# A graph layer on one core: the first edge layer as eight products of 32 rows and 64 columns, and 386 picked tiles instead of 376

## The chip, the core and the metric

The kernel runs on one core of a Trainium2 chip. A core has TensorE (matrix products, results in PSUM), VectorE (DVE), ScalarE (ACT), GpSimd (POOL) and queues that move data by DMA; each engine works through its own instructions in order and waits for others by semaphores. The metric is the device time of one execution in microseconds (us). Before the change it is 1485.16 us, the median of 7 runs (1483.39 to 1488.86).

## What is computed

```python
def ref(features, edge_index, edge_attr, edge_sh, c_noise, W1, b1, W2, b2, W_tp, ...):
    src, dst = edge_index                                    # 200000 edges, 6250 nodes, dst sorted
    w = silu(edge_attr @ W1 + b1) @ W2 + b2                  # 32 -> 64 -> 9 numbers an edge
    h_src = features[src]                                    # 64 numbers an edge
    msg = einsum('ef,em,fmg->eg', h_src, edge_sh * w, W_tp)
    agg = segment_sum(msg, dst, num_segments=N) / sqrt(AVG_DEG)
    gamma, beta = split(silu(c_noise[:, None] @ Wn1 + bn1) @ Wn2 + bn2, 2)
    return agg * (1.0 + gamma) + beta
out = layernorm(x + ref(x, ...))
```

## The kernel before

The 200000 edges are 1563 tiles of 128, in 98 groups of 16 tiles (`NBLK`, `KB`). The main loop runs over `i`, and works on several groups at once, each at another stage. The order of each engine's instructions is written out by hand: they stand as the code calls them.

**Features of the source nodes (`hs`).** A group needs 16 x 128 rows of `x`. Most tiles are fetched by `gather` (line 97): one indirect DMA a tile on POOL's queue (line 99), six groups ahead, into seven buffers. In each fourth group from 7 on one tile is fetched by SP, 128 single row copies (`load_rows`, line 107). The last `picked(g)` tiles of a group are not fetched at all but selected on TensorE out of a copy of `x` in SBUF: `hots` (line 533) builds one-hot matrices on DVE from keys in PSUM (which `keys`, line 528, copies on ACT), `pick` (line 540) multiplies them in 14 products into `px` (line 552), and DVE multiplies by a mask (line 561) and sums (line 563) into `hs`. `picked(g)` is 4, or 3 where `g` is a multiple of 6 below 96: 376 tiles in all, beside 23 by SP and 1164 gathers.

**Weights of the edges.** `hidden` (line 476) is the first layer: `ea` holds a group's edge attributes as 4 x 32 rows by 512 columns. Two products take 64 rows each, by a block-diagonal `w1bd` of two copies of `W1`, into the two banks of the PSUM tile `p1` (line 481). `hidden_act` takes the Silu of both banks in one activation (line 490) into `st`. `second` (line 494) is the second layer, four products with 32 output columns side by side (line 499) and an addition of the bias on ACT (line 502). `weights` (line 504) turns the result on DVE, multiplies by `sh` (line 513) and spreads it over seven windows of nodes into `a` (line 519).

**Edge sums.** `windows` (line 571) multiplies `hs` by `a`, tile by tile, 16 products of 64 columns in two halves of eight (line 585), each half into a PSUM tile `pz` of tag "pz" with two buffers; 252 of a bank's 512 columns are used. The first of these products waits for all gathers of the group. ACT copies the sums out (line 596). `project` (line 618) multiplies pairs of groups by `W_tp` into the PSUM tile that shares the tag "p1" with the first layer (line 632), turns the result (line 638) and splits it in two parts (lines 606, 607); `nodes` (line 666) with `place`, `bring`, `gate` and `finish` adds them up to nodes, in PSUM of tag "s", which `second` uses too.

**Order of an iteration.** `gather(i+6)`, loads, `keys(i+2)`; `pick(i+1, 0)` with the parts of `nodes(i)` and `hots(i+2)` between its products; `hidden(i+2)` (line 724); `second(i+1)`; `windows(i)`; `project` in odd iterations; `pick(i+1, 1)` with `weights(i+1)`; a part of the nodes' end; `pick(i+1, 2)`; `pick(i+1, 3)`. In the setup `hidden(0)` to `hidden(2)` are called out of the loop, and the tag "pz" also serves some small products.

```python
                pick(i + 1, 0, [nodes(i), more])
                ...
                if i + 2 < NBLK:
                    hidden(i + 2)
                ...
                second(i + 1)
                windows(i)
```

Of the kernel before, what the change touches and what calls it, by code (L numbers as in the profile page):

```python
# [7 lines left out]
F32 = mybir.dt.float32  # L8
# [4 lines left out]
AF = mybir.ActivationFunctionType  # L13
# [3 lines left out]
P = 128  # L17
N, F, M, D, H, E = 6250, 64, 9, 32, 64, 200000
NJ = 49
NPAD = P * NJ  # L20
NT = (E + P - 1) // P
KB = 16
NBLK = (NT + KB - 1) // KB
W = 7
KW = KB * W
ZT = 8
FB = 2
AHEAD = 6
LB = 2
Q = 4  # L30
J = 7
SPS = 4
SPG = range(7, NBLK, SPS)
# [17 lines left out]

def picked(g):

    return Q - (g % 6 == 0 and g < NBLK - LB)


def tiles(g):
# [10 lines left out]
def gnn_resnorm_kernel(ctx: ExitStack, tc: tile.TileContext, x, src, dst, dst_row, ea, sh, cn,  # L68
                       w1, b1, w2, b2, wtp, wn1, bn1, wn2, bn2, out):
    nc = tc.nc  # L70
# [6 lines left out]
    w1bd = consts.tile([P, 2 * H], F32)  # L77
    b1c = even(consts, P, 1, F32, name="b1c")
# [8 lines left out]
    with ExitStack() as fast:  # L87
        loads = fast.enter_context(tc.tile_pool(name="loads", bufs=3))
        work = fast.enter_context(tc.tile_pool(name="work", bufs=2))
        gath = fast.enter_context(tc.tile_pool(name="gath", bufs=AHEAD + 1))  # L90
        keep = fast.enter_context(tc.tile_pool(name="keep", bufs=1))
        psum = fast.enter_context(tc.tile_pool(name="psum", bufs=1, space=bass.MemoryType.PSUM))
        late = fast.enter_context(tc.tile_pool(name="late", bufs=2))

        hs, hs_dma = {}, {}

# [22 lines left out]
        w2p = keep.tile([P, D], F32)  # L119
# [50 lines left out]
                lambda: nc.vector.scalar_tensor_tensor(jl[:, c0:c1], kh, -float(J) / P, rest,  # L170
                                                       op0=ALU.mult, op1=ALU.add)]

        def keys_turn(g0, kf, tag, kt):

            c0 = g0 * Q
            p_kt = psum.tile([P, P], F32, tag=tag, name=f"p_kt{g0}", bufs=1 + (tag == "pz"))
            nc.tensor.transpose(p_kt, kf, ident)
            nc.scalar.copy(kt, p_kt)
            return lambda: nc.sync.dma_start(kd[c0:c0 + P, :], kt)
# [9 lines left out]
        KC = P // Q  # L189
        KN = 10 * KB  # L190

        def setup(temp):
# [19 lines left out]
            for c in range(KB // 4):  # L212
                q = c * D
# [44 lines left out]
            one = temp.tile([1, 1], F32)  # L258
            nc.vector.memset(one, 0.0)

            def keys_first(g, kf, tag):

                pk_t[g] = psum.tile([P, Q, P], F32, tag=tag, name=f"pk{g}", bufs=1 + (tag == "pz"))
                spread = []
                for t in range(picked(g)):
                    c = (g + 1) * Q - picked(g) + t
                    d0 = NBLK * KB + c * P
                    dg = xb.rearrange("p j f -> p (j f)")[:, d0:d0 + P]
                    nc.vector.tensor_scalar(dg, ident, kf[:, c:c + 1], None, op0=ALU.mult)
                    spread.append(lambda t=t, dg=dg: nc.tensor.matmul(pk_t[g][:, t, :], ones, dg,  # L270
                                                                      start=True, stop=True))
                return spread
# [6 lines left out]
            kb = [ztw[:, k * LB * Q:(k + 1) * LB * Q] for k in range(6)]  # L279
            for f in keys_of(0, LB, kb):  # L280
                f()
            for f in keys_first(0, kb[0], "pz"):
                f()
            spread = keys_first(1, kb[0], "r")
            pw_i = temp.tile([P, 1], I32)
            nc.vector.tensor_scalar(pw_i, pf, 147.0, None, op0=ALU.mult)
            nc.vector.tensor_scalar(pw_i, pw_i, 10, None, op0=ALU.logical_shift_right)
# [22 lines left out]
            pick(0, 2)  # L310
            hidden(1, act=False)
            kt = temp.tile([P, P], F16)
            keys_turn(LB, kb[0], "pz", kt)()
            hidden_act(1)
            load_keys(LB)
            p_row = psum.tile([len(SPG), P], F32, tag="pz", name="p_row", bufs=2)
            nc.tensor.transpose(p_row, row_f, ident)
            hots(1, 1, 2)
            pick(1, 0)
            nc.vector.tensor_copy(row_a, p_row)  # L320
            nc.vector.tensor_sub(rel[:, 0:2 * KB], dst_i[:, 0:2 * KB], row_i)
            near(0)
            p_f = psum.tile([KB, NBLK], F32, tag="pz", name="p_f", bufs=2)
            nc.tensor.matmul(p_f, first_t, ident[0:NBLK, 0:NBLK], start=True, stop=True)
            nc.scalar.copy(first_f, p_f)
            p_cn = psum.tile([P, NJ], F32, tag="pz", name="p_cn", bufs=2)
            nc.tensor.matmul(p_cn, cn_j, ident[0:NJ, 0:NJ], start=True, stop=True)
            cn_s = temp.tile([P, NJ], F32)
            nc.scalar.copy(cn_s, p_cn)
# [13 lines left out]
            hots(1, 2, 3)  # L343
            pick(1, 1)
            nc.vector.tensor_copy(lo, lo_i)
            p_nid = psum.tile([P, NBLK], F32, tag="pz", name="p_nid", bufs=2)
            nc.tensor.matmul(p_nid, sel[0:KB], first_f, start=True, stop=True)
            nc.vector.scalar_tensor_tensor(nid, p_nid, pw, lo, op0=ALU.add, op1=ALU.subtract)
            windows(0)
# [126 lines left out]
        def hidden(g, act=True):  # L476

            e = ea_t.pop(g)
            p1 = psum.tile([P, 2, KB * P // 4], F32, tag="p1", name=f"p1_{g}")
            for i in range(2):  # L480
                nc.tensor.matmul(p1[:, i, :].rearrange("p (c t e) -> p c t e", c=4, t=4), w1bd[i * 64:(i + 1) * 64, :],  # L481
                                 e[i * 64:(i + 1) * 64, :].rearrange("p (t c e) -> p c t e", t=4, c=4),
                                 start=True, stop=True)
            p1_t[g] = p1
            if act:
                hidden_act(g)

        def hidden_act(g):
            st[g] = work.tile([P, 2, KB * P // 4], F32, tag="st", name=f"st{g}")
            nc.scalar.activation(st[g], p1_t.pop(g), AF.Silu, bias=b1c)  # L490

        p2, p2s = {}, {}

        def second(g):

            s = st.pop(g)
            p2[g] = psum.tile([P, 2, 2 * P], F32, tag="s", name=f"p2_{g}")
            for c in range(KB // 4):
                nc.tensor.matmul(p2[g][c * D:(c + 1) * D, 0, :].rearrange("p (i e) -> p i e", i=2), w2p,  # L499
                                 s[:, :, c * P:(c + 1) * P], start=True, stop=True)  # L500
            p2s[g] = work.tile([P, 2 * P], F32, tag="p2s", name=f"p2s{g}")
            nc.scalar.activation(p2s[g], p2[g][:, 0, :], AF.Identity, bias=b2c)  # L502

        def weights(g):

            p, v = p2.pop(g), p2s.pop(g)

            def part():
                nc.vector.transpose(p[:, 1, :], v)  # L509
                sw = p[:, 0, 0:KB * M].rearrange("p (t m) -> p t m", m=M)  # L510
                sh = sh_t.pop(g)
                for i in range(2):
                    nc.vector.tensor_mul(  # L513
                        sw[:, 8 * i:8 * i + 8].rearrange("p (s c) m -> p s c m", s=2),
                        p[:, 1, i * P:(i + 1) * P].rearrange("p (c q) -> p c q", q=D)[:, :, 0:2 * M]
                        .rearrange("p c (s m) -> p s c m", s=2),
                        sh[:, 8 * i:8 * i + 8].rearrange("p (s c) m -> p s c m", s=2))
                a[g] = work.tile([P, KB, M, W], F32, tag="a", name=f"a{g}")
                nc.vector.tensor_mul(a[g], oh_t.pop(g)[:, :, None, :].to_broadcast([P, KB, M, W]),  # L519
                                     sw.unsqueeze(3).to_broadcast([P, KB, M, W]))  # L520

            return [part]
# [48 lines left out]
        def windows(g, k0s=None):  # L571

            nk = tiles(g)
            end = g == NBLK - 1
            hsg, ag = hs[g], a[g]
            z = zs[g] if g in zs else sums(g)


            for k0 in range(0, nk, ZT) if k0s is None else k0s:
                n = min(ZT, nk - k0)  # L580
                pz = [psum.tile([P, ZT // 2, M, W], F32, tag="pz", name=f"pz{g}_{k0}", bufs=2)]
                pz.append(psum.tile([P, ZT // 2, M, W], F32, tag="px", name=f"pz{g}_{k0}_", bufs=2) if end else pz[0])
                for k in range(n):
                    v = k % 2
                    mm = nc.tensor.matmul(pz[v][v * F:(v + 1) * F, k // 2].rearrange("p m w -> p (m w)"),  # L585
                                          hsg[:, k0 + k, :], ag[:, k0 + k].rearrange("p m w -> p (m w)"),
                                          start=True, stop=True)
                    if k0 + k == 0:

                        for d in hs_dma.pop(g)[(g not in SPG):]:  # L590
                            tc.add_manual_dep(mm.ins, d.ins.name, mybir.DependencyInfo(
                                mybir.DependencyClass.Sync, mybir.DependencyReason.DATA), reason="rows of the group")
                for v in range(2):
                    copy = nc.vector.tensor_copy if end and k0 == ZT and v == 1 else nc.scalar.copy
                    for h in range(2):
                        copy(  # L596
                            z[h * F:(h + 1) * F, 0:5 - h, k0 + v:k0 + n:2, :].rearrange("p m k w -> p k m w"),
                            pz[v][v * F:(v + 1) * F, 0:(n + 1 - v) // 2, h:M:2, :])
# [91 lines left out]
        with tc.manual_schedule(), tc.tile_pool(name="temp", bufs=1) as temp:  # L690
# [6 lines left out]
            for i in range(1, NBLK):  # L697
# [22 lines left out]
                    hots(i + 2, 2, Q)  # L720
                if 56 <= i <= 58:
                    reach(i - 56)
                if i + 2 < NBLK:
                    hidden(i + 2)
                if i == NBLK - 2:
                    break
                second(i + 1)
# [9 lines left out]
                for t in range(2, Q + 1):  # L737
                    for f in beside[(t - 2) * n:(t - 1) * n]:
                        f()
                    if t < Q:  # L740
                        pick(i + 1, t)
                    if t == 2 and ends:
                        ends.pop(0)()
                if i in (3, 5):
                    tables.append(keys_turn(LB + KC * (i - 1) // 2, kb[0], "s", kt))

            g = NBLK - 1
            q = NJ - 1
# [250 lines left out]
```

## Time and profile before

| what | value |
|---|---|
| median of 7 runs | 1485.16 us |
| the profiled execution | 1485.47 us, its span 1483.6 us |
| granted TensorE clock, mean | 0.991 |
| DVE line 537, one-hot matrices | 376 of 1082 ns |
| DVE lines 561 and 563, mask and sum | 376 of 677 and 620 ns |
| DVE idle before line 561, waiting for the picks | 217.3 us |
| TensorE idle before line 585, waiting for gathers | 12.9 us |
| ACT line 490, Silu of the first layer | 98 of 1114 ns |
| TensorE line 481, first layer | 392 records, 110.6 us busy |

The span runs from the first to the last instruction of one profiled execution. A line of a group gives source line, engine, operation, tiles, count, then busy time and the mean of one, then the idle time of the engine just before and what ended it. A TensorE record's length contains the way through the array, so records overlap, and what a stage costs is read from the starts of records. A line of a timeline gives start, length, engine, line, operation, tiles and count, with the idle time before it and its releaser in brackets.

### The profile page before, as it was taken

To read this page: it belongs to the slowest core of one execution; us is meant where nothing else is said; L and a number is where in the kernel's file an instruction comes from. 1 tells how busy PE (TensorE), PEld (TensorE's weight loads), DVE (VectorE), ACT (ScalarE), POOL (GpSimd) and SP (SyncE) were. 2 spreads that over 40 slices of the span, in tenths; PEclk is the share of its full clock that TensorE was granted. 3 is DMA by queue.
4 is the path that set the end of the run, shared out by engine and by line. 5 is a ranking of instruction groups with operands and counts; after the bars stand their busy time and mean duration, and the time that the engine had idled before them with its cause. 6 is when DMAs were issued, how large, how long until landed. Compare 5 with 4: busy or idle time off the path is not lost.

```text
span 1483.6 us, 34389 instructions
## 1 busy us (share of the span) xinstructions
PE 1448.4 (98%) x10929; PEld 1218.0 (82%) x10929; DVE 1209.5 (82%) x2194; ACT 514.0 (35%) x1323; POOL 1103.5 (74%) x1173
## 2 busy tenths in 40 slices
PE   7999999999999999999999999999999999999997
PEld 5788888888888888888888787887888878887886
DVE  8889888887988888878888788786888877977776
ACT  4323333342424333424333324242333332423322
POOL 7777777777777777777777777777777777777772
PEclk9999999999999999999999999999999999999999
DMA  6422232232222223222222222222322222222210
GB/s 194 105 68 58 57 83 56 56 84 57 56 59 81 56 57 79 60 57 56 74 61 55 55 64 71 54 55 53 81 55 53 62 73 53 56 55 78 55 28 18
DMA packets 90150, 95.98 MB, mean 65 GB/s; under 512 B 36696, under 2 KB 51242, under 8 KB 89962
## 3 DMA queue, kind: packets, MB, share of 16 engines
q0 software_dynamic: 37248, 38.22, 13.2%
q1 hardware_dynamic: 52138, 53.89, 12.1%
q8 instruction: 89, 1.46, 0.4%
q10 hardware_dynamic: 576, 1.61, 0.3%
q14 instruction: 99, 0.81, 0.2%
HBM read 91.88 MB, written 1.73 MB: 63 GB/s over the span
## 4 chain that ended last, share of the span: by engine, by line
PE 92%; DVE 3%; DMA 2%; POOL 1%; issue 1%; ACT 0%; SPq 0%; DVEq 0%; POOLq 0%; ACTq 0%
PE px L552 70%; PE pz L585 7%; PE p L481 7%; PE p L499 3%; PE pt L632 3%; DMA hs<-in_x_dram,src_i 2%; POOL hs L99 1%; PE ps L673 1%; DVE hot_k L537 1%; PE ps L648 1%; PE ps L663 1%; DVE xm L561 0%; PE pt L638 0%; DVE xs_w L277 0%; DVE hs L563 0%
## 5 line engine op out<-in xcount | busy, mean ns | idle before, releaser
L99 POOL DMA_INDIRECT hs<-in_x_dram,src_i x1164 | 1102.2, 947 | 356.5 <-issue 325.4
L552 PE MATMUL px<-xs_w,hot_k 128*128 128x448 f32 x5264 | 1134.0, 370 | 2.9 <-ACT xs_w L276 1.3
L552 PEld LDWEIGHTS px<-xs_w,hot_k 128*128 128x128 f32 x5264 | 969.3, 189 | 82.4 <-DVE xm L561 2.1
L561 DVE SCALAR_TENSOR_TENSOR xm<-li,jl,px 128x448 f32<-128x448 f32 x376 | 254.5, 677 | 220.4 <-PE px L552 217.3
L537 DVE TENSOR_TENSOR hot_k<-pk,nk 128x896 fp32r<-128x896 f32 x376 | 392.0, 1082 | 0.6 <-ACT pk L531 0.6
L490 ACT ACTIVATE st<-p,b1c 128x1024 f32<-128x1024 f32 x98 | 109.2, 1114 | 597.1 <-PE p L481 597.1
L563 DVE TENSOR_REDUCE hs<-xm 128x64 f32<-128x448 f32 x376 | 233.1, 620 | 12.9
L596 ACT COPY ztw<-pz 64x140 f32<-64x140 f32 (+1 forms) x780 | 209.0, 268 | 28.2 <-PE pz L585 13.2
L585 PEld LDWEIGHTS pz<-a,hs 128*64 128x64 f32 x3116 | 101.1, 139 | 55.7 <-issue 36.1
L585 PE MATMUL pz<-a,hs 128*64 128x63 f32 x3116 | 114.8, 227 | 15.2 <-DMA hs<-in_x_dram,src_i 12.9
L519 DVE TENSOR_TENSOR a<-oh,p 128x1008 f32<-128x1008 f32 x98 | 117.9, 1204 | 3.3
L481 PE MATMUL p<-ea,w1bd 64*128 64x512 f32 x392 | 110.6, 641 | 0.0
L654 ACT COPY carry<-ps 128x128 f32<-128x128 f32 x48 | 12.8, 266 | 203.5 <-PE ps L648 203.5
L499 PEld LDWEIGHTS p<-st,w2p 128*32 128x32 f32 x784 | 15.4, 108 | 72.7 <-issue 48.4
L499 PE MATMUL p<-st,w2p 128*32 128x256 f32 x784 | 62.6, 391 | 0.0
L531 ACT CAST pk<-kr 128x512 f32<-128x512 f16 (+1 forms) x96 | 54.7, 570 | 8.8 <-DVE hot_k L537 7.3
L632 PE MATMUL pt<-ztw,wtc 128*64 128x112 f32 x960 | 54.4, 259 | 0.0
L481 PEld LDWEIGHTS p<-ea,w1bd 64*128 64x128 f32 x392 | 29.5, 184 | 29.1 <-issue 28.0
L513 DVE TENSOR_TENSOR p<-p,sh 128x72 f32<-128x72 f32 x196 | 47.3, 241 | 6.7
L502 ACT ACTIVATE p2s<-p,b2c 128x256 f32<-128x256 f32 x98 | 45.8, 467 | 5.6 <-PE p L499 5.6
L632 PEld LDWEIGHTS pt<-ztw,wtc 128*64 128x64 f32 x960 | 46.6, 137 | 0.1
L509 DVE STREAM_TRANSPOSE p<-p2s 128x256 f32<-128x256 f32 x98 | 44.1, 450 | 0.0
(158 smaller groups left out, 458.7 us busy)
## 6 DMA issues: line engine op xcount, KB each, us to landing
hs<-in_x_dram SPq DMA_DIRECT2D x2944, 0.2 KB
ea<-in_ea_dram SPq DMA_DIRECT2D x48, 512.0 KB
hs<-in_x_dram,src_i POOLq DMA_INDIRECT x1164
kr<-kd SPq DMA_DIRECT2D x48, 256.0 KB
sh<-in_sh_dram SPq DMA_DIRECT2D x49, 144.0 KB
cb<-cn_d SPq DMA_DIRECT2D x12, 128.0 KB
out_dram<-o SPq DMA_DIRECT2D x23, 64.0 KB
dst_i<-in_dst_dram SPq DMA_DIRECT2D x1, 768.0 KB
```

Source lines behind the costliest of these rows:

```text
L99: hs_dma[g] = [nc.gpsimd.indirect_dma_start(out=hs[g][:, t - g * KB, :], out_offset=None, in_=x, in_offset=bass.IndirectOffsetOnAxis(ap=sr ...
L481: nc.tensor.matmul(p1[:, i, :].rearrange("p (c t e) -> p c t e", c=4, t=4), w1bd[i * 64:(i + 1) * 64, :], e[i * 64:(i + 1) * 64, :].rearra ...
L490: nc.scalar.activation(st[g], p1_t.pop(g), AF.Silu, bias=b1c)
L499: nc.tensor.matmul(p2[g][c * D:(c + 1) * D, 0, :].rearrange("p (i e) -> p i e", i=2), w2p, s[:, :, c * P:(c + 1) * P], start=True, stop=True)
L519: nc.vector.tensor_mul(a[g], oh_t.pop(g)[:, :, None, :].to_broadcast([P, KB, M, W]), sw.unsqueeze(3).to_broadcast([P, KB, M, W]))
L537: nc.vector.tensor_tensor(hot_k[g, t], pk_t[g][:, t, None, :].to_broadcast([P, J, P]), nk.unsqueeze(2).to_broadcast([P, J, P]), op=ALU.is_ ...
L552: nc.tensor.matmul(px.rearrange("p f l -> p (f l)"), hot_k[g, t][:, h, :], xs[i][:, h].rearrange("p f l -> p (f l)"), start=(h == 0 and i ...
L561: nc.vector.scalar_tensor_tensor(xm, li[:, None, :].to_broadcast([P, F, J]), jl[:, c:c + 1], px, op0=ALU.is_equal, op1=ALU.mult)
L563: nc.vector.tensor_reduce(hs[g][:, tiles(g) - q + t, :], xm, AX.X, ALU.add)
L585: mm = nc.tensor.matmul(pz[v][v * F:(v + 1) * F, k // 2].rearrange("p m w -> p (m w)"), hsg[:, k0 + k, :], ag[:, k0 + k].rearrange("p m w ...
L596: copy(z[h * F:(h + 1) * F, 0:5 - h, k0 + v:k0 + n:2, :].rearrange("p m k w -> p k m w"), pz[v][v * F:(v + 1) * F, 0:(n + 1 - v) // 2, h:M ...
L632: nc.tensor.matmul(pt[h * F:(h + 1) * F, 0, 0:KW], wtc2[:, c, :], z[h][:, c], start=(c == 0), stop=(c == 4))
```

## The change

The first layer becomes eight products a group: row group `q` of four (32 rows) by half `s` of two (256 edges' columns), each with a copy of `W1` of 64 columns. The row groups write to four banks: the lower halves of `p1`'s two banks, and the upper halves of the two banks of the edge sums. Those two banks are now tiles that live for the whole kernel (`pzw`), and the edge sums and the setup's small products use slices of them. The Silu takes three activations. `st`, `second` and `weights` follow the new order of edges. The call of `hidden(i + 2)` moves from ahead of `second(i + 1)` to behind `pick(i + 1, 2)`. `picked(g)` is 3 only where `g` is a multiple of 16: 386 picks, 1154 gathers.

```diff
 def picked(g):
-    return Q - (g % 6 == 0 and g < NBLK - LB)
+    return Q - (g % 16 == 0 and g < NBLK - LB)
...
+        pzw = [psum.tile([P, 4 * P], F32, tag=f"pz{i}", name=f"pzw{i}") for i in range(2)]
...
-            keys_turn(LB, kb[0], "pz", kt)()
+            keys_turn(LB, kb[0], kt, pzw[1][:, 0:P])()
...
-            p_row = psum.tile([len(SPG), P], F32, tag="pz", name="p_row", bufs=2)
+            p_row = pzw[0][0:len(SPG), 0:P]
...
         def hidden(g, act=True):
             e = ea_t.pop(g)
-            p1 = psum.tile([P, 2, KB * P // 4], F32, tag="p1", name=f"p1_{g}")
-            for i in range(2):
-                nc.tensor.matmul(p1[:, i, :].rearrange("p (c t e) -> p c t e", c=4, t=4), w1bd[i * 64:(i + 1) * 64, :],
-                                 e[i * 64:(i + 1) * 64, :].rearrange("p (t c e) -> p c t e", t=4, c=4),
-                                 start=True, stop=True)
+            p1 = psum.tile([P, 2, 4 * P], F32, tag="p1", name=f"p1_{g}")
             p1_t[g] = p1
+            half = [p1[:, 0, 0:2 * P], p1[:, 1, 0:2 * P], pzw[0][:, 2 * P:], pzw[1][:, 2 * P:]]
+            for s in range(2):
+                for q in range(4):
+                    nc.tensor.matmul(half[q][s * H:(s + 1) * H].rearrange("p (c t e) -> p c t e", c=4, t=2),
+                                     w1bd[q * D:(q + 1) * D, (q % 2) * H:(q % 2 + 1) * H],
+                                     e[q * D:(q + 1) * D].rearrange("p (s t c e) -> p s c t e", s=2, t=2, c=4)[:, s],
+                                     start=True, stop=True)
...
         def hidden_act(g):
-            st[g] = work.tile([P, 2, KB * P // 4], F32, tag="st", name=f"st{g}")
-            nc.scalar.activation(st[g], p1_t.pop(g), AF.Silu, bias=b1c)
+            st[g] = work.tile([P, 4, 2 * P], F32, tag="st", name=f"st{g}")
+            nc.scalar.activation(st[g][:, 0:2], p1_t.pop(g)[:, :, 0:2 * P], AF.Silu, bias=b1c)
+            for q in range(2):
+                nc.scalar.activation(st[g][:, 2 + q], pzw[q][:, 2 * P:], AF.Silu, bias=b1c)
...
-                nc.tensor.matmul(p2[g][c * D:(c + 1) * D, 0, :].rearrange("p (i e) -> p i e", i=2), w2p,
-                                 s[:, :, c * P:(c + 1) * P], start=True, stop=True)
+                nc.tensor.matmul(p2[g][c * D:(c + 1) * D, 0, :].rearrange("p (q e) -> p q e", q=4), w2p,
+                                 s[:, :, c * 2 * D:(c + 1) * 2 * D], start=True, stop=True)
...
-                pz = [psum.tile([P, ZT // 2, M, W], F32, tag="pz", name=f"pz{g}_{k0}", bufs=2)]
+                pz = [pzw[k0 // ZT][:, 0:ZT // 2 * M * W].rearrange("p (k m w) -> p k m w", m=M, w=W)]
...
-                if i + 2 < NBLK:
-                    hidden(i + 2)
                 if i == NBLK - 2:
                     break
                 second(i + 1)
...
                     if t < Q:
                         pick(i + 1, t)
+                    if t == 2 and i + 2 < NBLK:
+                        hidden(i + 2)
                     if t == 2 and ends:
                         ends.pop(0)()
```

More of the change, by code (lines that the diff above doesn't have):

```diff
@@ L171, in keys_of, with keys_turn @@
                                                        op0=ALU.mult, op1=ALU.add)]
-        def keys_turn(g0, kf, tag, kt):
+        def keys_turn(g0, kf, kt, p_kt=None):
             c0 = g0 * Q
-            p_kt = psum.tile([P, P], F32, tag=tag, name=f"p_kt{g0}", bufs=1 + (tag == "pz"))
+            if p_kt is None:
+                p_kt = psum.tile([P, P], F32, tag="s", name=f"p_kt{g0}")
             nc.tensor.transpose(p_kt, kf, ident)
@@ L259, in setup, with keys_first @@
             nc.vector.memset(one, 0.0)
-            def keys_first(g, kf, tag):
-                pk_t[g] = psum.tile([P, Q, P], F32, tag=tag, name=f"pk{g}", bufs=1 + (tag == "pz"))
+            def keys_first(g, kf, pk):
+                pk_t[g] = pk
                 spread = []
@@ L281, in setup @@
                 f()
-            for f in keys_first(0, kb[0], "pz"):
+            for f in keys_first(0, kb[0], pzw[0].rearrange("p (t e) -> p t e", t=Q)):
                 f()
-            spread = keys_first(1, kb[0], "r")
+            spread = keys_first(1, kb[0], psum.tile([P, Q, P], F32, tag="r", name="pk1"))
             pw_i = temp.tile([P, 1], I32)
@@ L322, in setup @@
             near(0)
-            p_f = psum.tile([KB, NBLK], F32, tag="pz", name="p_f", bufs=2)
+            p_f = pzw[1][0:KB, 0:NBLK]
             nc.tensor.matmul(p_f, first_t, ident[0:NBLK, 0:NBLK], start=True, stop=True)
             nc.scalar.copy(first_f, p_f)
-            p_cn = psum.tile([P, NJ], F32, tag="pz", name="p_cn", bufs=2)
+            p_cn = pzw[0][:, 0:NJ]
             nc.tensor.matmul(p_cn, cn_j, ident[0:NJ, 0:NJ], start=True, stop=True)
@@ L345, in setup @@
             nc.vector.tensor_copy(lo, lo_i)
-            p_nid = psum.tile([P, NBLK], F32, tag="pz", name="p_nid", bufs=2)
+            p_nid = pzw[1][:, 0:NBLK]
             nc.tensor.matmul(p_nid, sel[0:KB], first_f, start=True, stop=True)
@@ L513, in part @@
                     nc.vector.tensor_mul(
[L514 to L517, printed above, removed]
+                        sw.rearrange("p (q s t) m -> p q s t m", s=2, t=2)[:, :, i],
+                        p[:, 1, :].rearrange("p (q t d) -> p q t d", q=4, t=2)[:, :, :, i * M:(i + 1) * M],
+                        sh.rearrange("p (q s t) m -> p q s t m", s=2, t=2)[:, :, i])
                 a[g] = work.tile([P, KB, M, W], F32, tag="a", name=f"a{g}")
@@ L744, in gnn_resnorm_kernel @@
                 if i in (3, 5):
-                    tables.append(keys_turn(LB + KC * (i - 1) // 2, kb[0], "s", kt))
+                    tables.append(keys_turn(LB + KC * (i - 1) // 2, kb[0], kt))
             g = NBLK - 1
```

## The prediction

> **What bounds the kernel now.** I read the page's busy shares first, then its groups, the waits, and a timeline of one iteration.
>
> ```profile
> PE 1448.4 (98%) x10929; PEld 1218.0 (82%) x10929; DVE 1209.5 (82%) x2194; ACT 514.0 (35%) x1323; POOL 1103.5 (74%) x1173
> ...
> L99 POOL DMA_INDIRECT hs<-in_x_dram,src_i x1164 | 1102.2, 947 | 356.5 <-issue 325.4
> L552 PE MATMUL px<-xs_w,hot_k 128*128 128x448 f32 x5264 | 1134.0, 370 | 2.9 <-ACT xs_w L276 1.3
> ```
>
> Shares and the chain of waits (92% PE) say: TensorE alone. The POOL row contradicts them. Its 1164 gathers take 947 ns each, and the idle time before them is "issue" of 0.3 us, 1067 times in the list of waits: the cost of starting the next gather, not a wait for anybody. The first gather starts at 3.71 us and the last ends at 1459.69 + 0.94 = 1460.63, so (1460.63 - 3.71)/1164 = 1.2517 us each, without a pause. "74% busy" is a queue that never rests. TensorE meets it at the edge sums of line 585, which wait for their group's gathers:
>
> ```profile
> 827.26 0.94 POOL L99 DMA_INDIRECT hs<-in_x_dram,src_i  x1 [0.30 <-issue]
> 828.51 0.94 POOL L99 DMA_INDIRECT hs<-in_x_dram,src_i  x1 [0.30 <-issue]
> ```
> ```profile
> 830.98 1.15 PE L585 MATMUL pz<-a,hs 128*64 128x63 f32 x32 [3.26 <-DMA hs<-in_x_dram,src_i]
> 832.06 6.25 PE L552 MATMUL px<-xs_w,hot_k 128*128 128x448 f32 x22
> ```
> ```profile
> 828.00:830.00 2.00, 0.00 (x0) 0.00 (x0) 2.00 (x3) 0.68 (x2) 1.39 (x3) 1.00 1.05 387
> 830.00:832.00 2.00, 1.02 (x32) 1.04 (x32) 1.90 (x5) 0.29 (x2) 1.65 (x2) 1.00 0.17 35
> 832.00:834.00 2.00, 2.00 (x10) 1.77 (x6) 0.29 (x1) 1.92 (x8) 1.44 (x2) 0.51 0.16 27
> ```
>
> By counting gathers, group 54's last one ends at 828.20; its sums start at 830.98 after 3.26 us of idleness (columns of the third fence: stretch, length, busy time of PE, weight loads, DVE, ACT, POOL, then granted clock, DMA share, GB/s). The packets were slow because the block loads moved 387 GB/s at that moment. The same count for every group gives the lead of the gathers over the sums: 12.0 us at group 0, 8.1 at 18, 4.7 at 36, 2.6 at 42. Up to there TensorE is the slower of the two (14.75 us a group over groups 0 to 36, POOL 14.95) and eats the lead; from then on it waits (12.9 us before line 585 in the list of waits). So **two engines are at the bound**, TensorE in the first half and POOL in the second.
>
> The Trainium skill (TensorE: Matmul & The Clock Gate, "HAM oscillation") says that idle gaps over about 3.4 us halve the clock. The trace is harsher: after idle gaps of 3.26, 2.59, 3.31 and 3.33 us the clock is granted at 0.5 for 3.4 to 6.8 us. The group after the gap at 66 takes 17.4 us where its like take 15.5. By the rule these waits cost their length, 12.5 us; by the rows they cost about 6.5 us more. I take the rows. TensorE's own work is then 1483.6 - 12.9 - 6.5 = 1464.2 us.
>
> **The change part by part.**
>
> *First layer.* Now, in one iteration:
>
> ```profile
> 710.54 0.36 PE L552 MATMUL px<-xs_w,hot_k 128*128 128x448 f32 x1
> 710.83 0.70 PE L481 MATMUL p<-ea,w1bd 64*128 64x512 f32 x2
> ```
> ```profile
> 711.37 0.60 PE L481 MATMUL p<-ea,w1bd 64*128 64x512 f32 x2
> 711.89 0.42 PE L499 MATMUL p<-st,w2p 128*32 128x256 f32 x4
> ```
> ```profile
> 712.46 1.15 PE L585 MATMUL pz<-a,hs 128*64 128x63 f32 x32
> 713.54 9.08 PE L552 MATMUL px<-xs_w,hot_k 128*128 128x448 f32 x44
> ```
>
> Each f32 product stands as two records (two passes). The two row tiles of line 481 start together, in two rounds 0.53 us apart, and line 499 follows at 711.89: 1.06 us a group, of which 2 x 0.427 is streaming (512 columns at the 1.2 columns per ns that line 499 shows: second round 0.24 us after its first for 256 columns and a 32-column weight load) and the rest a weight load and the change of tile shape. Line 552 runs a record per 0.20 us, so line 481 came 0.09 us late: that is a change of shape.
>
> After, a product has 256 columns. If all eight tiles (four row groups times two column halves) run side by side, two rounds of 0.213 us, 0.05 us of weight load, some 0.05 us for eight starts 7 ns apart. But the stage moves from between pick 0 and the second layer, where shapes change anyway, to between two full-array picks. The Trainium skill (TensorEngine Tiling, "Key Properties") speaks against that: changing the tiling mode drains TensorE. Rows: 0.09 us into line 481, and out of line 585 into 552 0.09 plus a first record 0.1 us longer than its like. So 0.09 + 0.05 + 0.43 + 0.05 + 0.19 = 0.81 us against 1.06: **0.25 us less**, 98 times: 24.5 us. Without the rule (0.53 us) it would be 52 us; I take the rows of the drains. The trace shows two row tiles and four column tiles side by side, never eight of both kinds. The ends: 0.53 us (drains hidden), and 1.24 us if only four run at a time (two rounds more, 0.43), a loss of 0.18 us. The page "TensorE: Matmul & The Clock Gate" (Part 3) states that both kinds compose, and the four row groups have four banks of their own here; so I take eight.
>
> *Picks, 376 to 386.* A pick is 14 records of 0.20 us, 2.81 us: 10 more are +28.1 us on TensorE. They remove 10 gathers: 12.5 us of POOL. DVE gains 10 x (1082 + 677 + 620) ns = 24 us; it has 274 us idle, mostly waiting for picks.
>
> *Silu.* One activation of 1.11 us becomes one of 128x512 and two of 128x256. Nearest rows: line 531 (128x512) 0.57, line 502 (128x256) 0.47; together 1.51, so +0.4 x 98 = 39 us of ScalarE, which is 35% busy. The result is due at the second layer of the next iteration, after pick 3 and pick 0 (some 6.3 us). Queued behind it is the key copy for the next iteration: line 531 ran at 715.5 while its reader started at 724.6, 9 us later; the stage comes some 7 us later than now, so this cover shrinks to about 2 us less a square root's table loads (2 x 1.28 us, every fourth iteration). DVE's idle time is behind it. Cost nothing.
>
> *Second layer without the stage ahead of it.* It now follows pick 0 at once and needs the gates' PSUM read: line 403 ends at 710.17, pick 0's last record starts at 710.54. Still in time, by 0.6 us.
>
> *New waits.* The stage waits for the copies of line 596 from the lower halves (done at 715.6, stage due near 718) and for line 607's read of the shared tile (701.4, before pick 2 ends). Edge sums wait for the Silu reading the upper halves, 5 us earlier. Nothing. DVE's two products of line 513 keep their size (241 ns). Setup changes only slots; at most 2 us, taken up by the gathers' first lead of 12 us.
>
> **Sum.** TensorE alone: 1464.2 + 28.1 - 24.5 = 1467.8. POOL alone: group 96's last gather ends 7 x 1.2517 us before POOL's end, at 1451.87; ten fewer, 1439.35. Its landing: sums have started 2.1 us after the last gather without waiting (group 49) and 4.0 us after it with waiting (group 90), so they can start at 1441.5 to 1443.4. From line 585 of group 96 (1459.91) to the end 23.7 us remain, untouched: 1465.2 to 1467.1. The two are level. Stepping group by group with both rates (TensorE's measured interval changed by these terms; landing 2.3 or 4.0 us) gives 1467.6; the same model of before lacks 2.1 us against 1483.6, about half of which would return in after. So a span of 1468.6, and the profiled run has 1485.5 - 1483.6 = 1.9 outside: **1470.5 us**, 15 us below the profiled run (1485.5, 0.3 above the median).
>
> **Rivals.**
> - *Four at a time, slower.* Place: the first-layer stage. Eight products of 32 rows cost 1.24 us, and the ten picks are unpaid: 1464.2 + 28.1 + 98 x 0.18 = 1509.9, near 1512 us. It decides as soon as the stage costs over 0.97 us, since (1464.2 + 28.1 - 1483.6)/98 = 0.09 must be saved. For it: no row of eight. Against: lines 481 and 499.
> - *Drains dearer.* Stage at 0.9 to 0.97 us: 1464.2 + 28.1 less 98 x 0.16 to 0.09, with the 1.9 outside 1478 to 1485 us. For it: each drain was read off one row.
> - *The gathers are hidden.* With a stage of 0.53 us, TensorE alone would end at 1464.2 + 28.1 - 52 = 1440.3, 1442 us in all. Against: POOL's floor of 1465; it needs gathers that run faster than 1.25 us, of which no stretch shows any.
>
> **Numbers.** My case 0.66, most of it 1465 to 1478; four at a time (with other unforeseen stalls of that sign) 0.20; dearer drains 0.10, half of it within the bound; hidden gathers 0.04. The upper end reaches into the slower case. The runs shown spread so that about 0.2% (3 us) is what can be told from no change: faster 0.74, same 0.06, slower 0.20.
>
> **What would show it.** Right: 16 records of the stage start within 0.5 us, pick 3 begins about 0.8 us after the stage's first record; POOL still at 1.25 us a gather and ending near 1448; waits for the gathers only late and below 3 us, with few stretches at clock 0.5. Wrong: four starts per round in four rounds; POOL pausing for free buffers; the second layer or pick 3 waiting for DVE.

## The result, and the profile after

The changed kernel takes 1482.49 us (median of 24 runs, 1479.92 to 1485.95) against 1484.68 us of the kernel before (60 runs, 1480.2 to 1489.25). The ratio is 0.9986, with a 95% interval from 0.9979 to 0.9993: a small gain that can be told from none, where a gain of 1% was forecast. The profiled execution took 1479.96 us with a span of 1478.2, so it is one of the quickest of the 24.

The page of the kernel after (line 100 is the gather, 558 the picks, 486 the first layer, 506 the second layer, 591 the edge sums, 495 and 497 the Silu):

```profile
PE 1446.4 (98%) x12245; PEld 1226.1 (83%) x12245; DVE 1224.7 (83%) x2224; ACT 568.2 (38%) x1521; POOL 1095.6 (74%) x1163
...
L100 POOL DMA_INDIRECT hs<-in_x_dram,src_i x1154 | 1094.3, 948 | 353.3 <-issue 311.3
L558 PE MATMUL px<-xs_w,hot_k 128*128 128x448 f32 x5404 | 1183.6, 371 | 5.2 <-DVE xm L567 3.4
...
L591 PE MATMUL pzw<-a,hs 128*64 128x63 f32 x3116 | 113.0, 225 | 1.7 <-DVE nid L350 1.4
...
L506 PE MATMUL p<-st,w2p 128*32 128x256 f32 x784 | 62.6, 391 | 7.9 <-DVE xb L405 5.4
```

The edge sums no longer wait for gathers: 12.9 us of that are gone. POOL goes on as before and ends earlier; its last gather starts at 1448.55, 11.1 us sooner, where ten gathers of 1.25 us are worth 12.5. The gathers now lead the edge sums by 13 to 21 us from group 2 to the end, so TensorE alone sets the end. And there is something new in the last row: the second layer waits 7.9 us, all of it for DVE.

The new stage, in TensorE's timeline after:

```profile
700.24 0.36 PE L558 MATMUL px<-xs_w,hot_k 128*128 128x448 f32 x1
700.53 0.43 PE L486 MATMUL p<-ea,w1bd 32*64 32x256 f32 x2
700.54 0.43 PE L486 MATMUL pzw<-ea,w1bd 32*64 32x256 f32 x2
700.55 0.43 PE L486 MATMUL p<-ea,w1bd 32*64 32x256 f32 x2
700.57 0.43 PE L486 MATMUL pzw<-ea,w1bd 32*64 32x256 f32 x2
700.79 0.38 PE L486 MATMUL p<-ea,w1bd 32*64 32x256 f32 x2
...
701.14 0.47 PE L558 MATMUL px<-xs_w,hot_k 128*128 128x448 f32 x1
```

Eight records start within 0.05 us, the other eight 0.26 us later, and the next pick 0.61 us after the first. The first eight write `p`, `pzw`, `p`, `pzw`, two records each, the order of the eight products: all eight tiles run side by side. A pick's record at 700.24 would have been followed at 700.44: the way in costs 0.09 us, as the rows of before said.

What the new wait is stands in ScalarE's timeline from the end of iteration 47, which picks for group 48, one of the six groups with three picks:

```profile
747.28 0.30 ACT L820 ACTIVATE var<-var,eps 128x2 f32<-128x2 f32 x1 [3.90 <-DVE var L819]
747.60 1.28 ACT L495 ACT_TABLE_LOAD   x1
748.89 0.69 ACT L495 ACTIVATE st<-p,b1c 128x512 f32<-128x512 f32 x1
749.48 0.83 ACT L497 ACTIVATE st<-pzw,b1c 128x256 f32<-128x256 f32 x2
750.19 0.61 ACT L537 CAST pk<-kr 128x512 f32<-128x512 f16 x1
750.70 0.28 ACT L660 COPY carry<-ps 128x128 f32<-128x128 f32 x1
```
```profile
751.02 0.29 DVE L663 TENSOR_TENSOR yt<-ps,carry 128x128 f32<-128x128 f32 x1 [1.82 <-ACT carry L660]
751.23 0.21 DVE L404 TENSOR_SCALAR gam<-ps 128x64 f32<-128x64 f32 x1
751.36 0.21 DVE L405 TENSOR_TENSOR xb<-xb,ps 128x64 f32<-128x64 f32 x1
```
```profile
751.72 0.64 PE L506 MATMUL p<-st,w2p 128*32 128x256 f32 x8 [1.81 <-DVE xb L405]
```

The stage's second round starts by 746.02, but its Silu starts only at 748.89. Ahead of it in ScalarE's queue stands the square root of the nodes' end, waiting for DVE, and then the return to the Silu's table. (The Trainium skill, "ScalarE: Activation LUTs", "What ACT_TABLE_LOAD costs", gives 1283 ns and a further 1380 ns of drain for each switch; the load shows, the drain doesn't: the Silu follows at 1.29 us.) Behind the Silu stand the key copy and the carry copy (lines 537 and 660); DVE waits 1.82 us for the carry, the gates (lines 404 and 405) stand behind that, and the second layer needs the PSUM that they read. With a pick 3 of 2.8 us in between, this delay is covered. Without one, TensorE waits 1.8 us.

### The profile page after: what moved, and what is told of

The parts are those of the page before. It is cut to its first block, busy times and chain, and to the rows that moved or that the text cites. A ratio compares the mean times of both kernels' runs of the same rounds, so it can differ in the third digit from the quotient of the medians.

```text
span 1478.2 us, 37229 instructions
## 1 busy us (share of the span) xinstructions
PE 1446.4 (98%) x12245; PEld 1226.1 (83%) x12245; DVE 1224.7 (83%) x2224; ACT 568.2 (38%) x1521; POOL 1095.6 (74%) x1163
## 4 chain that ended last, share of the span: by engine, by line
PE 82%; DVE 6%; SPq 5%; issue 3%; POOL 1%; DMA 1%; ACT 1%; DVEq 0%; POOLq 0%; ACTq 0%
PE px L558 65%; PE pzw L591 6%; SPq L116 4%; PE p L506 3%; PE p L486 3%; PE pt L638 3%; DVE hot_k L543 1%; POOL hs L100 1%; DMA hs<-in_x_dram,src_i 1%; SPq L111 1%; DVE xm L567 1%; PE ps L679 1%; PE ps L654 1%; DVE a L525 0%; DVE hs L569 0%
## 5 line engine op out<-in xcount | busy, mean ns | idle before, releaser
L558 PE MATMUL px<-xs_w,hot_k 128*128 128x448 f32 x5404 | 1183.6, 371 | 5.2 <-DVE xm L567 3.4
L558 PEld LDWEIGHTS px<-xs_w,hot_k 128*128 128x128 f32 x5404 | 985.3, 189 | 118.6 <-issue 19.3
L602 ACT COPY ztw<-pzw 64x140 f32<-64x140 f32 (+1 forms) x780 | 209.7, 269 | 27.7 <-PE pz__25610 L591 5.9
L495 ACT ACTIVATE st<-p,b1c 128x512 f32<-128x512 f32 x98 | 67.5, 688 | 331.4 <-PE pzw L486 326.7
L591 PEld LDWEIGHTS pzw<-a,hs 128*64 128x64 f32 x3116 | 99.3, 138 | 41.8 <-issue 35.7
L591 PE MATMUL pzw<-a,hs 128*64 128x63 f32 x3116 | 113.0, 225 | 1.7 <-DVE nid L350 1.4
L497 ACT ACTIVATE st<-pzw,b1c 128x256 f32<-128x256 f32 x196 | 81.4, 470 | 0.0
L486 PE MATMUL p<-ea,w1bd 32*64 32x256 f32 x784 | 66.1, 400 | 0.0
L486 PE MATMUL pzw<-ea,w1bd 32*64 32x256 f32 x784 | 66.1, 400 | 0.0
L486 PEld LDWEIGHTS p<-ea,w1bd 32*64 32x64 f32 x784 | 21.5, 130 | 29.0 <-issue 18.0
```

Source lines behind the costliest of these rows:

```text
L486: nc.tensor.matmul(half[q][s * H:(s + 1) * H].rearrange("p (c t e) -> p c t e", c=4, t=2), w1bd[q * D:(q + 1) * D, (q % 2) * H:(q % 2 + 1) ...
L497: nc.scalar.activation(st[g][:, 2 + q], pzw[q][:, 2 * P:], AF.Silu, bias=b1c)
L558: nc.tensor.matmul(px.rearrange("p f l -> p (f l)"), hot_k[g, t][:, h, :], xs[i][:, h].rearrange("p f l -> p (f l)"), start=(h == 0 and i ...
L602: copy(z[h * F:(h + 1) * F, 0:5 - h, k0 + v:k0 + n:2, :].rearrange("p m k w -> p k m w"), pz[v][v * F:(v + 1) * F, 0:(n + 1 - v) // 2, h:M ...
```

## Experiments

The kernels of one comparison ran on one chip beside the kernel before, so across comparisons the ratios to before are the safer figures. Below, an interval is the time from the start of one group's edge sums to the next group's, read from line 591 (585 in the kernels from before).

### The 3-pick groups away from the square root

```diff
 def picked(g):
-    return Q - (g % 16 == 0 and g < NBLK - LB)
+    return Q - ((g == 0 or g % 16 == 2 and g > 2) and g < NBLK - LB)
```

The square root falls into iterations that leave 3 when divided by 4. A group of three that is a multiple of 16 always has one just ahead of it; one of the form 16k + 2 never has.

> The changed kernel with its six 3-pick groups at 0, 18, 34, 50, 66, 82 instead of 0, 16, 32, 48, 64, 80; still 386 picks and 1154 gathers. Theory: the 3-pick groups save only 0.9 to 1.5 us instead of a pick's 2.8 since there ScalarE is late: the square root's two table loads fall between the first layer and its Silu, and without pick 3 nothing covers them, so the second layer waits for ScalarE's carry copy. Off the iterations with a square root these five groups give back 1.9, 1.9, 1.9, 1.3, 1.3 us: 8 us less than the changed kernel, near 1474 us, and the waits of the second layer for DVE and ScalarE, 7.9 us, go to under 2. Rival: the stage that used to stand ahead of the second layer was the cover, and any 3-pick group stalls without it, square root or not: within 2 us of the changed kernel, 1481 to 1485.

Measured: 1471.81 us, ratio to before 0.9903 (0.9885 to 0.9920). Between the medians that is 10.7 us below the changed kernel, between the two profiled spans 7.7 (1478.2 and 1470.5); the intervals themselves give 8.2, of the 8 that were expected. The second layer's wait is gone from the list, and the five intervals are 12.6, 12.6, 12.6, 12.4 and 12.4 us where their like take 15.4 and 15.2: the full 2.8 of a pick. The same place in ScalarE's timeline, ahead of group 50:

```profile
771.98 0.69 ACT L495 ACTIVATE st<-p,b1c 128x512 f32<-128x512 f32 x1 [4.40 <-PE pzw L486]
772.57 0.83 ACT L497 ACTIVATE st<-pzw,b1c 128x256 f32<-128x256 f32 x2
773.28 0.61 ACT L537 CAST pk<-kr 128x512 f32<-128x512 f16 x1
773.83 0.27 ACT L660 COPY carry<-ps 128x128 f32<-128x128 f32 x1
```

The Silu now waits for TensorE alone, and the carry copy follows it within 1.9 us, with no square root or table ahead. The rival falls: a 3-pick group as such needs no cover.

### The square root behind the first layer

```diff
                 pick(i + 1, 1, [weights(i + 1), turn])
-                if ends:
+                if ends and (picked(i + 1) == Q or i % 4 != 3):
                     ends.pop(0)()
```

> The changed kernel with its 3-pick groups where it has them (0, 16, 32, 48, 64, 80), but in the five iterations ahead of them the nodes' middle part, with its square root, is called behind the first layer instead of ahead of it; the rest of the nodes' end moves into the next iteration. Theory: the Silu no longer stands behind the square root in ScalarE's queue, so the five 3-pick intervals go from 14.5 and 13.7 us to about 12.6 and 12.4 and the kernel to near 1474 us, within 3 us of the version with shifted groups. Rival: the groups shifted by two gained for another reason (the loads, the place against the row copies): within 2 us of the changed kernel, 1481 to 1485.

Measured: 1475.96 us, ratio 0.9948 (0.9933 to 0.9964). The time is 2 us above what was expected, and 4.2 above the shifted groups, where at most 3 were expected. The intervals say why: 13.7 three times and 13.4 twice, where 12.6 and 12.4 were expected; the second layer still waits 4.8 us in five places. The Silu is early now, but the square root and a table load still stand ahead of the carry copy:

```profile
741.65 0.69 ACT L495 ACTIVATE st<-p,b1c 128x512 f32<-128x512 f32 x1 [4.40 <-PE pzw L486]
742.23 0.83 ACT L497 ACTIVATE st<-pzw,b1c 128x256 f32<-128x256 f32 x2
743.09 1.28 ACT L820 ACT_TABLE_LOAD   x1
744.38 0.29 ACT L820 ACTIVATE var<-var,eps 128x2 f32<-128x2 f32 x1
744.58 0.58 ACT L537 CAST pk<-kr 128x512 f32<-128x512 f16 x1
745.10 0.26 ACT L660 COPY carry<-ps 128x128 f32<-128x128 f32 x1
```

So 0.8 us (three times) and 0.3 us (twice), 3 us in all, is what the Silu's place costs, and the rest is the square root's own place in the queue. The other 3 us between this kernel's profiled span, 1472.1, and the changed kernel's came from the setup (below). The two experiments together put the stall on ScalarE's queue, but on all that is ahead of the carry copy, not on the Silu alone.

### The changed kernel with the picks of before

```diff
-    return Q - (g % 16 == 0 and g < NBLK - LB)
+    return Q - (g % 6 == 0 and g < NBLK - LB)
```

> The changed kernel with the 376 picks and 1164 gathers of before. TensorE alone would end 28 us sooner than in the changed kernel, less some 4 us of stalls in more 3-pick groups: a span near 1454. Theory: then POOL sets the end. Its floor for 1164 gathers is 12.5 us above that for 1154, a span of 1478 to 1480, and the waits for gathers return, with stretches at clock 0.5: 1480 to 1486 us, no better than the changed kernel. Rival: gathers can be hidden once the stage is short: near 1458 us.

Measured: 1486.44 us, ratio 1.0001 (0.9990 to 1.0012), half a microsecond above the range that was expected. The short stage alone brings nothing. TensorE waits for the gathers again, more than before, and the clock pays for it:

```profile
PE pzw L591 <- DMA hs<-in_x_dram,src_i: 16.5, 9, 4.2
PE p L506 <- DVE xb L405: 7.7, 4, 2.2
```
```profile
828.00:830.00 2.00, 0.03 (x4) 0.00 (x0) 1.97 (x4) 0.47 (x1) 1.39 (x3) 0.99 1.00 330
830.00:832.00 2.00, 0.37 (x7) 0.40 (x9) 2.00 (x3) 0.00 (x0) 1.58 (x2) 0.50 0.50 165
832.00:834.00 2.00, 2.00 (x32) 1.88 (x29) 1.90 (x4) 1.16 (x5) 1.50 (x2) 0.50 0.21 38
```

(First the list of TensorE's waits: us in total, times, longest; then stretches with the granted clock third from the end.) The floor of POOL is real: 1164 gathers end at 1462.8, and the span ends 22.2 us later, at 1485.0. The kernel also carries its own control: the intervals to the 3-pick groups 24, 36 and 48, which follow a square root, take 14.5 to 14.9 us, those to groups 18 and 30, which don't, 12.6. (Others of this kernel mix with other waits.)

### The kernel before with 386 picks

```diff
-    return Q - (g % 6 == 0 and g < NBLK - LB)
+    return Q - (g % 16 == 0 and g < NBLK - LB)
```

> The kernel before with 386 picks (3 only where the group is a multiple of 16) and 1154 gathers, all else as before. Theory: TensorE's own work of 1464.2 us grows by ten picks of 2.81 us and hides the gathers: a span of 1492, near 1494 us, no waits for gathers, and 3-pick intervals 2.8 us shorter than their like, since the two-tile stage still stands ahead of the second layer and its Silu ahead of the square root. The stage of eight products is then worth 1494 - 1482.5 + the 8 us of stalls, some 20 us. Rival: the picks are cheap since waits for gathers go: at or below 1484.

Measured: 1489.85 us, ratio 1.0042 (1.0026 to 1.0059), a span of 1487.9 with no wait for gathers. Its 3-pick intervals are 12.9 and 12.7 us against 15.7 and 15.5: the full pick, at the very groups where the changed kernel stalls. It measures TensorE's own work, 1487.9 - 28.1 = 1459.8 us, 4.4 less than was taken. Interval by interval it also measures the stage: over 87 of the 97 intervals the changed kernel is 0.246 us shorter on average. (Left out are the first two, the five short ones and those from groups 56, 95 and 96.) The interval from group 95 gives the stage itself: in the changed kernel it holds the last stage and takes 15.21 us, here it holds none and takes 14.40. So eight products cost 0.81 us.

### The first layer in its old place

```diff
+                if i + 2 < NBLK:
+                    hidden(i + 2)
                 if i == NBLK - 2:
                     break
                 second(i + 1)
...
-                    if t == 2 and i + 2 < NBLK:
-                        hidden(i + 2)
```

> The changed kernel with the first layer called where it stood before, ahead of the second layer. Theory: changes of tile shape cost 0.2 us less per group there, but the edge sums then follow 0.6 us behind the second layer and must wait for the Silu to leave their banks (three activations, 1.5 us, whole-bank dependence): 1.1 us of waiting against 0.2 us saved, 0.9 x 96 = 86 us more than the changed kernel, near 1565 us. Rival: other columns of a bank are independent, nothing waits, and TensorE saves 19 us and the square-root stalls: POOL's floor, 1467 to 1470 us.

Measured: 1520.33 us, ratio 1.0247 (1.0231 to 1.0263). The wait is there, in each group, but smaller than expected:

```profile
710.73 0.64 PE L506 MATMUL p<-st,w2p 128*32 128x256 f32 x8
711.98 1.15 PE L591 MATMUL pzw<-a,hs 128*64 128x63 f32 x32 [0.61 <-ACT st L497]
```

The edge sums wait for the Silu although it reads other columns of their banks. An iteration takes 0.5 us more than with the stage behind pick 2 (15.9 against 15.4, 14.6 against 14.1), not 0.9: the wait is 0.6 us as TensorE counts it, and the changes of shape give back 0.1. So the move is what makes the shared banks usable. It is also what made the stall: here, with the same eight products and three activations, the 3-pick groups take 13.1 and 12.9 us where their like take 15.9 and 15.7, the full pick again.

### The setup

```diff
-            p_row = pzw[0][0:len(SPG), 0:P]
+            p_row = p2[0][0:len(SPG), 1, 0:P]
```

> The changed kernel, with the setup's transposed row numbers in the unused half of the second layer's PSUM tile instead of in the first of the two long-lived banks. Theory: in the setup TensorE waits 1.31 us for the Silu and 1.22 us for a copy out of that bank, although they touch other columns, because the bank is one tile; the idleness also drops the clock to 0.5 for 3.4 us. Without it the first edge sums start near 33 us instead of 36.2, and as TensorE alone sets the end, all of it arrives there: 3 us less, near 1479.5. Rival: the gathers set the end, or a later stall takes it up: no change, 1482.5 within 1.

Measured: 1480.35 us, ratio 0.9962 (0.9948 to 0.9976). The two waits are gone and the first edge sums start at 32.3 us instead of 36.2. But their second half then waits 2.34 us for another copy where it waited 1.36, and by the sums of group 3 the kernel is at 83.2 us against 83.9. Most of the difference is taken up by the clock: up to there this execution ran 10.2 us at clock 0.5, the changed kernel's 6.8. Less half of these stretches it is 78.1 against 80.5 us.

Both edits, the shifted groups and this one, in one kernel:

> Both edits together. Theory: they are separate stalls of TensorE and add up: 8 + 3 us less than the changed kernel, near 1471.5, with the lead of the gathers over the edge sums at the end down from 13.9 us to about 4, still without long waits. Rival: POOL's floor, a span of 1465.2 to 1467.1, holds sooner than thought: not below 1475.

Measured: 1472.21 us (1468.94 to 1476.63), ratio 0.9912 (0.9896 to 0.9928): no different from the shifted groups alone, though its own sums of group 3, less half of 3.4 us at clock 0.5, stand at 78.8. At the end the gathers lead by 4.7 us, so POOL's floor is near (span 1467.2, the forecast floor 1465.2 to 1467.1). Whether the some 2 us that the mended setup saves by group 3 arrive at the end stays open. What the traces do show is a scatter in the setup: by the sums of group 3 the executions with the same setup stand at 83.9 and 83.6 us (the changed kernel, shifted groups) or at 80.6 (376 picks, square root behind). The first two have two stretches of 3.4 us at clock 0.5 before 70 us, the others none; half of 6.8 us is 3.4, and 3.0 to 3.3 us lie between them. The kernel before was at 80.1, without such a stretch.

## Why the prediction was wrong

**The forecast.** 1470.5 us, a gain of 15 us; measured 1482.49, a gain of 2. The direction held; the time lies above the 1465 to 1478 us where most of the chance had been put.

**What bounds the kernel: right.** Two engines at the bound was the reading, against a chain of waits that gave 92% to TensorE. The stage alone gave 1.0001, the picks alone 1.0042, both together 0.9986, and with the stall away 0.9903: each half is worthless without the other. One sentence of that reading is the wrong way round: with 14.75 us a group against 14.95, TensorE is the faster of the two over groups 0 to 36, and this is why the gathers' lead shrinks. That the block loads slowed the packets was not tested.

**The stage: right.** Eight tiles side by side, and 0.246 us less a group where 0.25 was worked out from the drains on the rows and 0.53 would have come without them.

**TensorE's own work: 4.4 us too high,** as the before-with-386 run shows. The waits for gathers were taken with 12.9 us and their slow stretches with 6.5. In the trace of before the four stretches at clock 0.5 last 20.5 us in all; half of that is 10.2, 3.7 more than was taken. The forecast lost little by it, since POOL's floor stood beside it.

**"Cost nothing" for the Silu: the step that failed.** It counted pick 3 and pick 0 as the cover of ScalarE's queue and named the square root's two table loads, "every fourth iteration", but it didn't ask what happens in the groups that have no pick 3, and these are all in iterations with a square root. The second layer's margin of 0.6 us behind the gates was read off an iteration with all four picks too; in the short ones it becomes a wait of up to 1.8 us for these same gates, the sign that the text itself had named. In the five intervals the changed kernel loses 1.64 us three times, 1.03 and 1.06 against the kernel before with the same picks, where it should gain 0.246 each: (3 x 1.64 + 1.03 + 1.06) + 5 x 0.246 = 8.2 us. The intervals of the shifted groups gave back the same 8.2 us.

**"Setup ... taken up by the gathers' first lead": failed too.** A lead of the gathers hides a late POOL, not a late TensorE, and the sum of the same text had TensorE level with POOL. In the profiled execution the sums of group 3 start 3.8 us later than before, though they come behind five stages of 0.81 us instead of six of 1.06, which should be 2.3 us sooner. So the setup costs 6.1 us. 3.4 of them are the clock. The other 2.7 are waits, more than the "at most 2" of the text: from 14 to 75 us TensorE's waits add up to 7.8 us, 5.2 before. The longest is a pick 3 that waits for DVE:

```profile
61.38 5.09 PE L558 MATMUL px<-xs_w,hot_k 128*128 128x448 f32 x16 [2.21 <-DVE xm L567]
```

**The sum, put right.** 1459.8 + 28.1 - 98 x 0.246 + 8.2 + 6.1 = 1478.1 us; the span is 1478.2. This is the profiled execution; the median is 2.5 us longer, at a mean clock of 0.995 instead of 0.997. Without the stall and with a clock at full in the setup the sum is 1466.5, level with POOL's floor: the shifted groups' 1471.81 us is near what had been forecast for the change itself.

**The rivals.** Four at a time fell with the eight records of one round. Hidden gathers fell with the run of 376 picks. Dearer drains, a stage at 0.9 to 0.97 us, had the right time for the wrong reason: the stage costs 0.81.

## What to carry to other kernels

Two engines that are level give nothing for a gain on one: pay for a shorter stage with work taken off the other engine, and measure each half alone. When a stage is moved, follow its consumer through each queue in the iteration that is shortest, not in the usual one; a pattern of exceptions (every sixteenth group) against a pattern of events (every fourth iteration) can meet always or never, and here moving it by two was worth more than the change itself: 8.2 us of intervals, against a gain of 2 us.

## What the runs showed of the hardware

Idle times shorter than the 2.59 us seen before can also be followed by half of TensorE's clock, but the length alone doesn't decide it. In the changed kernel a wait of 2.2 us near 60 us was followed by 3.4 us at 0.5, its waits of 1.8 us for the second layer were not. In the shifted groups' kernel the same pick waits as long, and the clock stays full:

```profile
62.73 3.48 PE L558 MATMUL px<-xs_w,hot_k 128*128 128x448 f32 x16 [2.24 <-DVE xm L567]
```
```profile
63.00:66.00 3.00, 3.00 (x16) 2.81 (x16) 1.70 (x4) 0.00 (x0) 2.38 (x3) 1.00 0.19 34
```

In the kernel with the mended setup waits of 2.07 and 1.80 us, before the second layers that precede the edge sums of groups 32 and 48, were followed by half clock (third figure from the end):

```profile
514.38 0.64 PE L506 MATMUL p<-st,w2p 128*32 128x256 f32 x8 [2.07 <-DVE xb L405]
```
```profile
512.00:515.00 3.00, 0.93 (x12) 0.23 (x10) 1.31 (x4) 1.66 (x5) 2.39 (x3) 1.00 0.75 175
515.00:518.00 3.00, 3.00 (x39) 2.77 (x37) 2.96 (x5) 2.60 (x9) 2.09 (x3) 0.57 0.64 213
```
```profile
753.23 0.64 PE L506 MATMUL p<-st,w2p 128*32 128x256 f32 x8 [1.80 <-DVE xb L405]
```
```profile
754.00:757.00 3.00, 3.00 (x37) 2.73 (x34) 2.97 (x5) 2.54 (x9) 2.08 (x4) 0.55 0.60 200
```

A wait of 2.13 us at 275 us of the same execution was not. What decides it stays open. Times go with the clock: of the changed kernel's executions, those with a mean clock of 0.997 took 1479.96 to 1480.50 us, those with 0.992 took 1484.96 to 1485.95. A gather kept its 1.25 us on POOL in every kernel, whatever the other engines did.
